# Two state space stages with one scan per unit instead of two and the product a unit ahead, and the preparation around them rearranged

## The chip, the cores and the metric

The kernel runs on one core of a Trainium2 chip. The metric is the device time of one execution in microseconds (us): the median of three runs before is 2466.05 us, from 2464.59 to 2468.78.

The core has five engines with a queue each: TensorE (PE, with its weight loads shown as PEld), VectorE (DVE), ScalarE (ACT), GpSimd (POOL) and SyncE (SP), which here issues the DMAs. Matmul results land in PSUM, eight banks of 128 partitions by 512 floats; everything else is in SBUF.

## The reference, cut to what matters

A stack of 16 layers works on x, 4 batches by 512 positions by 128 channels in float32; each adds f(layernorm(x)) to x. The order is L0a, L0f, L0b, L0f, L1a, L1f, L1b, L1f, L2a, L2f, L2b, L2f, L3a, L3f, L3b, L3f. Three places matter here.

L2b and L3b are state space layers (256 inner channels, 16 states each):

```python
xi, z = in_proj(x)                       # 256 + 256 channels
u = silu(causal_conv4(xi) + conv_b)
dtr, Bc, Cc = split(u @ x_proj)          # 64, 16, 16
delta = softplus(dtr @ dt_proj + dt_proj_b)
A = -exp(A_log)
def step(h, inp):                        # over the 512 positions
    d_t, b_t, c_t, u_t = inp
    dA = jnp.exp(d_t[:, :, None] * A)
    h = dA * h + (d_t * u_t)[:, :, None] * b_t[:, None, :]
    y = jnp.einsum('bdn,bn->bd', h, c_t)
    return (h, y)
y = (y + u * D) * silu(z)
return y @ out_proj
```

L0b is an attention with 16 heads of 8 that weighs all keys once, takes the mean weight of every key over all queries, keeps the 391 keys of 512 with the largest mean (the last 64 always) and attends again over these alone. L2f is a mixture of experts, and L3f a small gated layer; the two are touched only where they hold the beginning of the state space layer that follows.

## The kernel before

Everything is written out in Python, engine by engine. A matmul with `pin=True` and an instruction in `keep(...)` stay in the order in which they are written on their engine; others can be moved by the scheduler between those. The line numbers are those of the profile.

**The loop of L2b and L3b** (`mamba`, L2143). A unit holds 16 inner channels with their 16 states: 8 channels by 16 states fill the 128 partitions, and the two halves t = 0 and 1 lie side by side, each with 512 positions. A batch has 16 units (the two groups c of 128 channels, 8 units each), and a stage 64, numbered n over the four batches. For each unit:

- `fetch` (L2262): two DMAs on SP's queue copy delta from DRAM into a `da` tile, every row of 512 positions spread to 16 partitions. It runs five units ahead, into one of six tiles.
- `decay` (L2273): two ACT instructions make exp(delta * A) in `da`, three units ahead. For the first three units delta comes from PE (`spread`) through a PSUM bank instead of a DMA.
- `gain` (L2284): four matmul records on PE spread delta * u into two PSUM banks, `ps_du`, one unit ahead; there are two such pairs.
- `scan` (L2291): on DVE the product of `ps_du` with B (L2293, 128 x 1024), and then one scan for each half (L2298, 128 x 512), h = da * h + ps_du, from zero; then on GpSimd the product with C (L2301, 128 x 1024), which for the very last unit is on DVE.
- `read` (L2305): every second round, for two units, eight matmul records gather the states into `ps_y`, four units behind.
- `gated` (L2325) on DVE multiplies a group's `ps_y` with silu(z); `output` (L2328) projects a batch back, and `add_to_x` (L440) adds it and takes the moments of the next layernorm.

PSUM holds two pairs of `ps_du`, two banks of tag y and two of tag mm, the last for all other matmuls.

**The preparation of a batch** (`prepare`, L2166) makes u, silu(z), delta, delta * u, B and C of the next batch while this one runs. It is a generator: the loop takes one piece of it in a round (L2363), from round 1 for batch 1 and from two rounds before the end of a batch's 16 for the others. Four pieces are the convolution; then come u and the first half of the gate, the projection to dtr, and one piece with both softplus halves on ACT and eight products of 128 x 512 on GpSimd (L2242) with the DMAs of delta to DRAM behind each four; then B, C and the second half of the gate.

**The first batch** is prepared in the layer before (`mamba_ahead`, L1973): in L2f by a table of rounds (L1943 to L1967), in L3f by hand at its end (L2764 to L2791). `step`, `log` and `rest` are the softplus of one half c; `self.late` lists what runs inside the loop's first rounds instead. In L2f the spare tiles for it are quarters of `xn`, in L3f the second set of batch tiles. `norm` is `roots` (a Sqrt on ACT and a reciprocal) and `centred` (L393, four instructions of 128 x 128 on DVE per batch). `prime` loads an ACT table by a dummy instruction.

**L0b** (L745). In 68 rounds the first pass runs: `weights(n)`, and behind it `importance(n - 4)`, which sums the weights of the keys. `choose(0)` (L879) picks the keys of the first two batches in 16 steps on DVE (a max of 8 and a replace each, L897 and L899), one in a round by a pattern of the round numbers, and sends a mask into the rows of `k` by DMA. `largest(n, i)` (L912) takes the largest score of the second pass (a matmul and a `tensor_reduce`, L925, with four i to a tile n); `into_q` (L974) puts the maxima of four tiles into `q`. In rounds 64 to 66 the first three tiles run; the rest is the start of `stream`, the list of the second pass, whose `weigh` needs `into_q`.

Of the kernel before, what the change touches and what calls it, by code (L numbers as in the profile page):

```python
# [11 lines left out]
F32 = mybir.dt.float32  # L12
# [6 lines left out]
P = 128  # L19
# [255 lines left out]
class Net:  # L275
# [469 lines left out]
    def L0b(self):  # L745
# [7 lines left out]
        with ExitStack() as es:  # L753
# [178 lines left out]


# [12 lines left out]
            AHEAD = 3  # L946
            for n in range(64 + LATE):
# [7 lines left out]
                if 64 <= n < 64 + AHEAD:  # L955
                    for i in range(4):
                        largest(n - 64, i)
# [7 lines left out]
                if n < 36 or n % 7 < 4:  # L965
                    next(choice, None)
            for _ in choice:
                pass
            choice = choose(1)

            def into_q(n):  # L974

                b, g, _ = split(n)
                nm = nmt[n // 4 % 2]
                pt = bank("ps_t", (P, CB, P))
                for j in range(CB):
                    self.tr(pt[:, j], nm[:, j].rearrange("p i r -> p (i r)"))  # L980
                qb = q[g][:, b * S : b * S + S]
                keep(
                    nc.vector.tensor_tensor(qb, qb, pt.rearrange("p j t -> p (j t)"), ALU.add)  # L983
                )
# [75 lines left out]
            LAG = 5  # L1060
            stream = [(largest, n, i) for n in range(AHEAD, LAG) for i in range(4)]
# [19 lines left out]

            plan.at(4 * (4 - AHEAD) + 4, into_q, 3)
            for m in range(len(stream) + 20):
                plan.run(m)
                if m < len(stream):
                    f, n, i = stream[m]
                    f(n, i)
                    if f is largest and i == 3:
                        next(choice, None)
# [807 lines left out]
    def L2f(self):  # L1897
# [3 lines left out]
        with (  # L1901
# [36 lines left out]
            if f:  # L1938

                def bank(name):  # L1940
# [4 lines left out]
                    for at, n, *a in (  # L1945
# [8 lines left out]
                        (30, "step", 1),  # L1954
                        (30, "log", 0),
                        (30, "log", 1),
                        (31, "rest", 0),
                        (32, "rest", 1),
                        (34, "br"),
                        (35, "cr"),  # L1960
                        (37, "gate", 0),
                        (38, "gate", 1),
# [5 lines left out]
                self.late = ((0, f["norm"], 3, 4), (2, f["turn"], 3))  # L1968
# [4 lines left out]
    def mamba_ahead(self, g, spare):  # L1973
# [21 lines left out]
        if spare:  # L1995

            e0, w0, l0, e1 = (
                self.xn[:, CB * b : CB * b + CB].rearrange("p j d -> p (j d)") for b in range(B)
            )
        else:  # L2000
            m["sets"][1] = self.mamba_set(sp, 1)
            e0, w0, l0, e1 = (m["sets"][1][i][:, c] for i in range(2) for c in range(2))
        e, wl, ln = (e0, e1), (w0, sz[:, 0]), (l0, sz[:, 1])
# [65 lines left out]
        def step(c, bank):  # L2069
# [5 lines left out]
            keep(nc.scalar.activation(e[c], ps, AF.Abs, bias=db))  # L2075
            keep(nc.scalar.activation(e[c], e[c], AF.Exp, scale=-1.0))

        def log(c, bank):


            keep(nc.scalar.activation(ln[c], e[c], AF.Ln, bias=ones[:, 0:1]))
            keep(nc.vector.tensor_scalar(wl[c], e[c], 1.0, None, ALU.add))
            keep(
                nc.vector.scalar_tensor_tensor(
                    wl[c], wl[c], 1.0, e[c], ALU.subtract, ALU.subtract
                )
            )

        def rest(c, bank):
            for o, x, y, op in (  # L2090
                (ln[c], ln[c], wl[c], ALU.subtract),
                (dl[:, c], dl[:, c], ln[c], ALU.add),
# [17 lines left out]
            "log": log,  # L2110
# [32 lines left out]
    def mamba(self, g):  # L2143

        nc, tc = self.nc, self.tc
        LAG, AHEAD, FETCH = 4, 3, 5
        with ExitStack() as es:
# [13 lines left out]
            def bank(name):  # L2163
                return pp.tile([P, S], F32, tag="mm", name=name, bufs=2)

            def prepare(b):  # L2166
# [4 lines left out]
                for c in range(2):  # L2171
# [7 lines left out]
                    yield  # L2179

                def gate():
                    raw = rp.tile([P, 2, S], F32, tag="t", name="raw")
                    for c in range(2):
                        ps = bank("ps_z")
                        self.mm(
                            ps,
                            w["in"][:, 256 + c * P : 256 + c * P + P],
                            xT[:, xb : xb + S],
                            pin=True,
                        )  # L2190
                        nc.scalar.copy(raw[:, c], ps)
                        if c == 0:
                            yield
                    nc.scalar.activation(sz, raw, AF.Silu)
                    yield

                nc.scalar.activation(u, raw, AF.Silu)
                gates = gate()
                next(gates)
# [17 lines left out]
                yield  # L2217

# [15 lines left out]
                nc.scalar.activation(w1, w1, AF.Identity, bias=ones[:, 1:2])  # L2234
                for c in range(2):
                    for o, x, y, op in (
                        (w1, w1, e, ALU.subtract),
                        (ln, ln, w1, ALU.subtract),
                        (dl, dl, ln, ALU.add),
                        (du, dl, u, ALU.mult),  # L2240
                    ):
                        nc.gpsimd.tensor_tensor(o[:, c], x[:, c], y[:, c], op)  # L2242
                    nc.sync.dma_start(dram[b][:, c], dl[:, c])
                yield
                yield
                project(br, 64, P)
# [598 lines left out]
```

## Time and profile before

| what | us |
|---|---|
| median of three runs (2464.59 to 2468.78) | 2466.05 |
| the profiled execution, in all | 2471.9 |
| its span in the trace | 2470.2 |
| PE, DVE, ACT, POOL busy in the span | 2183.7, 1751.5, 1307.5, 608.9 |
| L0b, about 498 to 943 | 445 |
| L2f before L2b, 1435 to 1616 | 181 |
| L2b, 1616 to 1875 | 259 |
| L3f before L3b, 2106 to 2169 | 63 |
| L3b, 2169 to 2431 | 262 |

The chain that ended last gives 61% of the span to PE and 26% to DVE, by lines 9.6% to the scans of L2298 and 4.1% to the product of L2293. In the 40 slices PE is at 7 to 9 tenths nearly everywhere, which tells little, since its ends are modelled; DVE is at 9 only in the two state space stages, and GpSimd too is busiest there.

How to read the lines below: a group's line has busy time, the mean of one in ns, and the idle time of the engine before them with what ended it. A timeline line has the start, the duration, and in brackets the idle time before it. A line of windows has the stretch, its length, and the busy time of PE, PEld, DVE, ACT and POOL, then the granted clock of PE and the share and rate of the DMAs. A wait's line has who waited for whom, the total, the times and the longest.

### The profile page before, as it was taken

How to read it: one execution, taken by the hardware profiler on the slowest of the kernel's cores; microseconds unless marked ns; L12 is line 12 of the kernel's file. 1: busy time of each engine (PE TensorE's matmuls, PEld its weight loads, DVE VectorE, ACT ScalarE, POOL GpSimd, SP SyncE). 2: the span in 40 equal slices, each digit the busy share in tenths (PEclk: the TensorE clock that was granted, in tenths of full speed). 3: DMA queues.
4: the chain of work that ended last, by engine and by line, in shares of the span. 5: the costliest groups of instructions: out<-in, count | busy, mean ns of one | idle time of the engine just before them, and what ended most of it. 6: DMA issues, size and time to landing. Idle time of an engine off the chain costs nothing.

```text
span 2470.2 us, 32491 instructions
## 1 busy us (share of the span) xinstructions
PE 2183.7 (88%) x11647; PEld 1025.6 (42%) x11647; DVE 1751.5 (71%) x3544; ACT 1307.5 (53%) x2561; POOL 608.9 (25%) x431
## 2 busy tenths in 40 slices
PE   7999999999899998899877789888868998888867
PEld 2343334733233443567434345442214566422213
DVE  6666666689887675656464674579997557589995
ACT  4555554279645555342442464667635445478642
POOL 1100010010000001022152410048761015148761
PEclk9999999999799999999867889999979999989888
DMA  3000002300000000510200033235542420045540
GB/s 141 1 1 1 1 1 68 72 1 1 2 1 2 1 1 1 112 27 7 100 1 1 0 67 75 56 111 162 148 125 56 87 48 2 1 119 153 152 131 17
DMA packets 68304, 126.79 MB, mean 51 GB/s; under 512 B 9264, under 2 KB 13360, under 8 KB 67504
## 3 DMA queue, kind: packets, MB, share of 16 engines
q1 hardware_dynamic: 68144, 124.73, 19.4%
q8 instruction: 92, 1.51, 0.2%
q14 instruction: 68, 0.56, 0.1%
HBM read 118.93 MB, written 5.64 MB: 50 GB/s over the span
## 4 chain that ended last, share of the span: by engine, by line
PE 61%; DVE 26%; ACT 5%; DMA 3%; issue 2%; POOL 1%; SPq 0%; DVEq 0%; POOLq 0%; ACTq 0%
PE ps_o L346 13%; PE ps_s L346 11%; DVE hc L2298 10%; PE ps_st L346 5%; PE ps_c L346 4%; PE ps L346 4%; DVE ps_du L2293 4%; PE ps_g L346 4%; PE ps_u L346 2%; PE ps_v L346 2%; PE ps_x L346 2%; PE ps_qk L346 2%; DVE xn L393 2%; DVE e L839 2%; PE ps_q L346 2%
## 5 line engine op out<-in xcount | busy, mean ns | idle before, releaser
L2301 POOL TENSOR_TENSOR hc<-hc,cr 128x1024 f32<-128x1024 f32 x126 | 296.0, 2362 | 202.3 <-DVE hc L2298 134.7
L2298 DVE TENSOR_TENSOR_SCAN hc<-da,ps_du 128x512 f32<-128x512 f32 x256 | 298.2, 1206 | 15.6 <-ACT da L2282 2.6
L346 PE MATMUL ps_s<-k,q 32*128 32x512 f32 (+3 forms) x1088 | 275.8, 611 | 16.5 <-DVE mx L839 8.6
L346 PE MATMUL ps_du<-du,spread 64*128 64x512 f32 x512 | 167.5, 730 | 100.3 <-DVE hc L2298 97.9
L538 ACT ACTIVATE e<-ps_s,mx 128x512 f32<-128x512 f32 x256 | 172.6, 686 | 139.9 <-DVE mx L533 133.3
L2282 ACT ACTIVATE da<-da,am 128x512 f32<-128x512 f32 x244 | 165.3, 716 | 96.6 <-DMA da<-dram 82.5
L925 DVE TENSOR_REDUCE nm<-ps_s 128x1 f32<-128x512 f32 x256 | 160.4, 683 | 69.6 <-PE ps_s L346 67.8
L346 PE MATMUL ps<-xT,w_L2f 128*128 128x512 f32 (+1 forms) x416 | 197.1, 621 | 4.0 <-DVE t L1932 4.0
L1007 ACT ACTIVATE e<-ps_st 128x512 f32<-128x512 f32 x256 | 135.3, 601 | 104.9 <-PE ps_s L346 92.4
L533 DVE TENSOR_REDUCE mx<-ps_s 128x2 f32<-128x1024 f32 x128 | 150.9, 1219 | 43.8 <-PE ps_s L346 43.6
L346 PE MATMUL ps_st<-q,k 32*128 32x512 f32 x512 | 167.3, 632 | 6.5 <-DVE q L983 5.5
L2293 DVE TENSOR_TENSOR ps_du<-ps_du,br 128x1024 f32<-128x1024 f32 x128 | 154.8, 1210 | 12.4 <-PE ps_du L346 12.4
L850 ACT ACTIVATE e<-e,mx 128x512 f32<-128x512 f32 (+3 forms) x256 | 140.2, 549 | 20.6 <-DVE mx L839 20.0
L346 PEld LDWEIGHTS ps_s<-k,q 32*128 32x128 f32 x1088 | 96.5, 198 | 113.1 <-DVE mx L839 52.7
L346 PEld LDWEIGHTS ps_du<-du,spread 64*128 64x128 f32 x512 | 46.0, 209 | 214.2 <-DVE hc L2298 184.5
L346 PE MATMUL ps_s<-q,k 64*128 64x512 f32 x512 | 129.1, 618 | 2.2 <-ACT e L538 1.7
L346 PE MATMUL ps_c<-e,vz 128*64 128x512 f32 x512 | 123.5, 604 | 0.8 <-POOL vz L549 0.8
L1932 DVE SCALAR_TENSOR_TENSOR t<-ps,w_L2f,t 128x512 f32<-128x512 f32 (+1 forms) x104 | 76.8, 746 | 63.5 <-PE ps L346 44.4
L346 PEld LDWEIGHTS ps<-xT,w_L2f 128*128 128x128 f32 (+1 forms) x416 | 76.6, 193 | 101.4 <-issue 75.2
L839 DVE CUSTOM_DVE_ANT_0 e<-ps_s,tri 128x512 f32<-128x512 f32 (+3 forms) x256 | 109.6, 484 | 10.1 <-PE ps_s L346 10.1
L1931 ACT ACTIVATE t<-ps,w_L2f 128x512 f32<-128x512 f32 (+1 forms) x104 | 69.7, 682 | 87.3 <-PE ps L346 84.4
L549 POOL TENSOR_TENSOR vz<-v,z 128x512 f32<-128x512 f32 x32 | 33.4, 1043 | 322.0 <-DVE z L547 293.0
(505 smaller groups left out, 4235.1 us busy)
## 6 DMA issues: line engine op xcount, KB each, us to landing
da<-dram SPq DMA_DIRECT2D x244, 256.0 KB
wt<-dram SPq DMA_DIRECT2D x144, 128.0 KB
wt<-dram SPq DMA_DIRECT2D x32, 256.0 KB
dram<-dl SPq DMA_DIRECT2D x16, 256.0 KB
wt<-dram SPq DMA_DIRECT2D x16, 224.0 KB
wt<-dram SPq DMA_DIRECT2D x16, 192.0 KB
wt<-dram SPq DMA_DIRECT2D x16, 160.0 KB
w_L2f<-w_L2f SPq DMA_DIRECT2D x1, 2433.0 KB
```

Of the source, the lines that this page charges most:

```text
L346: i = self.nc.tensor.matmul(out, lhsT, rhs, start=start, stop=stop)
L533: nc.vector.tensor_reduce(mx, sc, AX.X, ALU.max, negate=True)
L538: nc.scalar.activation(es[n][:, hh], sc[:, hh], AF.Exp, bias=mx[:, hh : hh + 1], accum_out=z[m][:, j, hh : hh + 1],)
L839: red = nc.vector.tensor_tensor_reduce(e[:, i, :w], sc[i][:, :w], tri[:, S - w :], -1.0, BIG, ALU.add, ALU.min, mx[:, i : i + 1],)
L850: nc.scalar.activation(e[:, i, :w], e[:, i, :w], AF.Exp, bias=mx[:, i : i + 1], scale=-1.0, accum_out=z[:, i : i + 1],)
L925: nc.vector.tensor_reduce(nm[:, j, i, 9:10], sc, AX.X, ALU.max, negate=True)
L1007: keep(nc.scalar.activation(es_[n][:, i], sc, AF.Exp))
L1932: nc.vector.scalar_tensor_tensor(t[:n], p3[:n], b3[:n, m : m + 1], t[:n], ALU.add, ALU.mult)
L2282: keep(nc.scalar.activation(da[n][:, t], src, AF.Exp, scale=am[:, at : at + 1]))
L2293: nc.vector.tensor_tensor(dx[n], dx[n], sets[b % 2][4].unsqueeze(1).to_broadcast([P, 2, S]), ALU.mult)
L2298: nc.vector.tensor_tensor_scan(hc[n][:, t], da[n][:, t], dx[n][:, t], 0.0, ALU.mult, ALU.add)
L2301: (nc.vector if n == 16 * B - 1 else nc.gpsimd).tensor_tensor(hc[n], hc[n], sets[b % 2][5].unsqueeze(1).to_broadcast([P, 2, S]), ALU.mult)
```

## The change

In the loop, `product` is taken out of `scan` and issued for unit n + 1 ahead of scan n; `gain` runs two units ahead, and there are three pairs of `ps_du`. The two scans become one over 1024 positions: the six `da` tiles are made once, the first position of their second half is set to zero, and the DMA and the exponential leave it out (511 positions), so that the state begins anew there. mm and y have one PSUM bank each. Two units instead of three are spread by PE. The last `roots` of L2b and all `centred` calls move ahead of the loops.

`prepare` has 16 pieces: B before the softplus, GpSimd's products one to a piece with C, the gate and its silu between them, the DMA of a half behind its third product, and delta * u as the last two. The loop takes two pieces in rounds 0, 2, 4, 6 and 8, none in round 1, and one otherwise; later batches begin four rounds before the end of a batch.

In L2f the softplus of both halves is joined (`exps`, `logs`) and spread over rounds 30 to 41. In L0b `choose(0)` has a faster pattern, the first five tiles of `largest` run in rounds 62 to 66 with `into_q(3)` among them, and `choose(1)` makes its first part before the stream and goes on from stream position 16.

```diff
+                if 62 <= n < 62 + LAG:
+                    largest(n - 62, 0)
+                    if n == 66:
+                        into_q(3)
+                    for i in range(1, 4):
+                        largest(n - 62, i)
...
-                if n < 36 or n % 7 < 4:
+                if n < 36 or n % 3 < 2:
                     next(choice, None)
...
             choice = choose(1)
+            next(choice)
...
-            stream = [(largest, n, i) for n in range(AHEAD, LAG) for i in range(4)]
+            stream = []
...
-                    if f is largest and i == 3:
+                    if f is largest and i == 3 and m >= 16:
                         next(choice, None)
...
-                        (30, "step", 1),
-                        (30, "log", 0),
-                        (30, "log", 1),
-                        (31, "rest", 0),
-                        (32, "rest", 1),
-                        (34, "br"),
-                        (35, "cr"),
-                        (37, "gate", 0),
-                        (38, "gate", 1),
+                        (31, "step", 1),
+                        (32, "br"),
+                        (33, "exps"),
+                        (34, "cr"),
+                        (36, "logs"),
+                        (37, "rest", 0),
+                        (38, "rest", 1),
+                        (40, "gate", 0),
+                        (41, "gate", 1),
...
-                self.late = ((0, f["norm"], 3, 4), (2, f["turn"], 3))
+                self.late = ((2, f["turn"], 3),)
...
+        def exps(bank):
+            keep(nc.scalar.activation(e, e, AF.Exp, scale=-1.0))
+            self.prime(AF.Silu)
+
+        def log(e, wl, ln, by_act=False):
+            if by_act:
+                keep(nc.scalar.activation(wl, e, AF.Identity, bias=ones[:, 0:1]))
+            else:
+                keep(nc.vector.tensor_scalar(wl, e, 1.0, None, ALU.add))
+            keep(nc.scalar.activation(ln, e, AF.Ln, bias=ones[:, 0:1]))
+            keep(nc.vector.scalar_tensor_tensor(wl, wl, 1.0, e, ALU.subtract, ALU.subtract))
+
+        def logs(bank):
+            log(e, wl, ln)
+            self.prime(AF.Silu)
...
-        LAG, AHEAD, FETCH = 4, 3, 5
+        LAG, SPREAD, AHEAD, FETCH = 4, 2, 3, 5
...
-                return pp.tile([P, S], F32, tag="mm", name=name, bufs=2)
+                return pp.tile([P, S], F32, tag="mm", name=name)
...
+                steps = (
+                    (w1, w1, e, ALU.subtract),
+                    (ln, ln, w1, ALU.subtract),
+                    (dl, dl, ln, ALU.add),
+                )
                 for c in range(2):
-                    for o, x, y, op in (
-                        (w1, w1, e, ALU.subtract),
-                        (ln, ln, w1, ALU.subtract),
-                        (dl, dl, ln, ALU.add),
-                        (du, dl, u, ALU.mult),
-                    ):
+                    for k, (o, x, y, op) in enumerate(steps):
                         nc.gpsimd.tensor_tensor(o[:, c], x[:, c], y[:, c], op)
-                    nc.sync.dma_start(dram[b][:, c], dl[:, c])
-                yield
-                yield
-                project(br, 64, P)
-                yield
-                project(cr, 192, P)
-                yield
-                for _ in gates:
+                        if k == 2:
+                            nc.sync.dma_start(dram[b][:, c], dl[:, c])
+                        if (c, k) == (0, 1):
+                            project(cr, 192, P)
+                        if (c, k) == (0, 2):
+                            gate(1)
+                        if (c, k) == (1, 0):
+                            nc.scalar.activation(sz, z, AF.Silu)
+                        yield
+                for c in range(2):
+                    nc.gpsimd.tensor_tensor(du[:, c], dl[:, c], u[:, c], ALU.mult)
                     yield
...
+            ring = [sp.tile([P, 2, S], F32, name=f"da{n}") for n in range(6)]
+            for t in ring:
+                nc.gpsimd.memset(t[:, 1, 0:1], 0.0)
+            da = {n: ring[n % 6] for n in range(16 * B)}
...
-                        da[n][:, t],
-                        dram[b][8 * m : 8 * m + 8, c].unsqueeze(0).to_broadcast([16, 8, S]),
+                        da[n][:, t, t:],
+                        dram[b][8 * m : 8 * m + 8, c, t:].unsqueeze(0).to_broadcast([16, 8, S - t]),
...
-                dx[n] = pp.tile([P, 2, S], F32, tag="du", name="ps_du", bufs=2)
+                dx[n] = pp.tile([P, 2, S], F32, tag="du", name="ps_du", bufs=3)
...
+            def product(n):
+                br = sets[n // 16 % 2][4].unsqueeze(1).to_broadcast([P, 2, S])
+                keep(nc.vector.tensor_tensor(dx[n], dx[n], br, ALU.mult))
+
             def scan(n):
-                b = n // 16
-                nc.vector.tensor_tensor(
-                    dx[n], dx[n], sets[b % 2][4].unsqueeze(1).to_broadcast([P, 2, S]), ALU.mult
-                )
                 hc[n] = rp.tile([P, 2, S], F32, name="hc", bufs=7)
-                for t in range(2):
-                    nc.vector.tensor_tensor_scan(
-                        hc[n][:, t], da[n][:, t], dx[n][:, t], 0.0, ALU.mult, ALU.add
-                    )
+                h, a, x = (t.rearrange("p t s -> p (t s)") for t in (hc[n], da[n], dx[n]))
+                keep(nc.vector.tensor_tensor_scan(h, a, x, 0.0, ALU.mult, ALU.add))
...
+            if g == "L2b":
+                self.roots(B - 1, B, keep)
+            self.prime(AF.Exp)
             gain(0)
-            for n in range(AHEAD):
-                da[n] = rp.tile([P, 2, S], F32, name="da", bufs=6)
-                decay(n)
-            for n in range(AHEAD, FETCH):
+            decay(0)
+            gain(1)
+            product(0)
+            if g == "L2b":
+                self.centred(B - 1, keep)
+            decay(1)
+            for n in range(SPREAD, FETCH):
                 fetch(n)
+            decay(2)
...
+            pace = {0: 2, 1: 0, 2: 2, 4: 2, 6: 2, 8: 2}
             for n in range(16 * B + 10):
                 if n + FETCH < 16 * B:
                     fetch(n + FETCH)
+                if n + 1 < 16 * B:
+                    product(n + 1)
                 if n < 16 * B:
                     scan(n)
-                if n + 1 < 16 * B:
-                    gain(n + 1)
+                if n + 2 < 16 * B:
+                    gain(n + 2)
                 if n + AHEAD < 16 * B:
                     decay(n + AHEAD)
-                b, k = divmod(n + 2, 16)
+                b, k = divmod(n + 4, 16)
                 if k == 0 and 1 < b + 1 < B:
                     ahead = prepare(b + 1)
-                if n >= 1:
+                for _ in range(pace.get(n, 1)):
                     next(ahead, None)
...
-                        plan.at(n if last else n + 2, gated, m // 16, m // 8 % 2)
+                        plan.at(n if last else n + 1, gated, m // 16, m // 8 % 2)
...
                 f["step"](0, bank)
+                self.centred(2, keep)
                 f["log"](0, bank)
...
                 f["cr"](bank)
+                self.centred(3, keep)
                 f["turn"](1, bank)
                 self.late = (
-                    (0, lambda bank: self.centred(2, keep)),
                     (0, f["step"], 1),
-                    (0, f["log"], 1),
-                    (0, f["rest"], 1),
-                    (1, lambda bank: self.centred(3, keep)),
+                    (1, f["log"], 1),
+                    (1, f["rest"], 1),
                     (2, f["turn"], 2),
-                    (3, f["turn"], 3),
-                    (4, f["gate"], 0),
-                    (5, f["gate"], 1),
+                    (4, f["turn"], 3),
+                    (5, f["gate"], 0),
+                    (6, f["gate"], 1),
                 )
```

## The prediction

> **What bounds the kernel now.** I read the 40 slices first (counted from 0, DVE is at 9 tenths in slices 27 to 29 and 36 to 38, the two state space stages), then the costliest groups, then DVE's timeline inside a stage, then the waits.
>
> ```profile
> L2298 DVE TENSOR_TENSOR_SCAN hc<-da,ps_du 128x512 f32<-128x512 f32 x256 | 298.2, 1206 | 15.6 <-ACT da L2282 2.6
> L2293 DVE TENSOR_TENSOR ps_du<-ps_du,br 128x1024 f32<-128x1024 f32 x128 | 154.8, 1210 | 12.4 <-PE ps_du L346 12.4
> ```
>
> The product and the scans have almost no idle time before them: DVE sets the pace of both loops. The timeline (start, duration) gives a unit, first in steady state, then in a place where the order happened to differ:
>
> ```profile
> 1664.68 1.21 DVE L2293 TENSOR_TENSOR ps_du<-ps_du,br 128x1024 f32<-128x1024 f32 x1
> 1666.02 2.33 DVE L2298 TENSOR_TENSOR_SCAN hc<-da,ps_du 128x512 f32<-128x512 f32 x2
> 1668.27 1.21 DVE L2293 TENSOR_TENSOR ps_du<-ps_du,br 128x1024 f32<-128x1024 f32 x1
> ...
> 1839.16 1.23 DVE L2293 TENSOR_TENSOR ps_du<-ps_du,br 128x1024 f32<-128x1024 f32 x1
> 1840.30 4.54 DVE L2298 TENSOR_TENSOR_SCAN hc<-da,ps_du 128x512 f32<-128x512 f32 x4
> 1844.76 1.21 DVE L2293 TENSOR_TENSOR ps_du<-ps_du,br 128x1024 f32<-128x1024 f32 x1
> ```
>
> A unit takes 1668.27 - 1664.68 = 3.59: from product to its own scan 1.34, scans to next product 2.25. At 1839 the scan behind the product belongs to an earlier one, and the step is 1.14; the four scans take 4.46, or 2.23 a pair.
>
> The other engines, by windows (length, then PE, PEld, DVE, ACT, POOL busy, clock), and PE's waits in the first of the loops:
>
> ```profile
> 1684.55:1865.60 181.05, 138.31 (x514) 38.82 (x512) 175.89 (x181) 101.39 (x136) 132.77 (x65) 0.86 0.45 131
> 2198.00:2242.00 44.00, 37.00 (x127) 10.46 (x129) 37.91 (x34) 38.07 (x49) 31.38 (x19) 0.96 0.49 137
> PEld ps_du L346 <- DVE hc L2298: 93.0, 49, 3.6
> ```
>
> From unit 16 on only DVE is full (97%). PE waits for a scan at 49 of 64 units, 1.9 us each: that is its slack. At the start of the second loop ACT (87%) is as full as DVE, and DVE stalls.
>
> **Part 1, the loops from unit 16 to 62.** The product of unit n+1 now stands before scan n, so no scan follows its own product: 1.14 in place of 1.34. One scan of 1024 replaces two of 512; no row shows one. From rows: a 1024 product is 1.210 and a 512 one (gated, L2326) 0.675, so a fixed 0.14 and 0.535 per 512; a 512 scan is 1.206, so 1.066 of streaming; a joint one 2.13 + 0.14 = 2.27, and less the overlap of 0.09 (1.206 against 1.115 from start to start) 2.18 to the next start. Bounds: 2.13 (streaming alone) and 2.25 (nothing gained). I take 2.18. New unit 1.14 + 2.18 = 3.32, or 0.27 less. 94 units in the two loops; in some 12 of them gated or a moments instruction already stands between product and scan, and they gain 0.05: 82 x 0.27 + 12 x 0.05 = **-22.7** (bounds -16 and -27).
>
> [...]
>
> **Part 2, what that cover hides no longer.** PE: mm and y banks fall from two to one each, since three products need six. A matmul into mm now waits until ACT has emptied it (0.6 to 0.7 by L2176, L2191, L2214; 1.3 more if a pair of decays stands before it on ACT). Behind that matmul, in PE's order, stand read and the next gain, and DVE's next product waits for gain. Cover: 1.9 per unit. In a batch's eight busy units (1739.8 to 1768.4 of PE's timeline) gain takes 1.06, each projection or convolution piece 1.9 to 1.98, read 1.06 in every second unit: some 28.5 us, against 8 x 3.59 = 28.7 now and 8 x 3.32 = 26.6 then. It is 1.9 short, about one unit's slack; at the reduced clock seen at 1785 (gain 2.08, not 1.13) more. Four such batches: **+4** (0 to +14).
>
> ACT needs 42.6 per 60.3 in a whole batch, 80% of the new 53. GpSimd needs 16 x 2.36 + 8 x 1.28 = 48.0 of 53.1; spreading its 8 preparation products one to a unit keeps hc's backlog near 8 x 0.32 = 2.6, where they ran 10 us in one piece. A piece that waits for ACT's softplus chain holds hc products behind it, and read on PE, four units late by design (13 us), waits for those. On SP the writes of dl stand among the fetches and wait for GpSimd; a fetch issued at 1728.67 landed at 1732.25 for a scan at 1748.19, 14 us of cover. The rows of 511 elements, four bytes off, have no row: even twice the 3.6 us stays under it. All three at 0.
>
> **Part 3, start of the first loop.** Scan 0 starts at 1620.93 and scan 16 at 1684.55, 63.6 for 16 x 3.59 + 0.6 = 58.0. Gain(1) stood on PE behind six spreading matmuls and their evictions (product 1 waited 4.8); now it follows gain(0), and two units are spread, not three. Roots moves ahead of the loop: moments end at 1617.99, then a Sqrt load 1.28, 0.30, an Exp load 1.28, prime 0.20, both decays 1.3: scan 0 at 1622.5. Scan 16 at 1622.5 + 53.1 + 0.6 = 1676.2, a gain of 8.3. The preparation runs two pieces in units 0, 2, 4, 6 and 8, so some stall comes back: **-6** (0 to -8).
>
> **Part 4, start of the second loop.** Scan 0 at 2170.93, scan 16 at 2243.41: 72.5, 14.5 over 58.0. Where it goes:
>
> ```profile
> 2173.18 3.19 DVE L393 TENSOR_SCALAR xn<-x,ln_mv,ln_rs 128x128 f32<-128x128 f32 x4
> 2180.89 2.37 DVE L393 TENSOR_SCALAR xn<-x,ln_mv,ln_rs 128x128 f32<-128x128 f32 x1
> 2216.33 1.23 DVE L2293 TENSOR_TENSOR ps_du<-ps_du,br 128x1024 f32<-128x1024 f32 x1 [3.18 <-PE ps_du L346]
> ```
>
> Eight centred instructions take 7.1 there beside GpSimd (four take 1.09 where GpSimd is idle, 2159.64). They move before the loop, 1.1 into a wait of 1.42 for ACT and 1.1 into one of 1.37 for PE: nothing, or +2.2 without that cover. The waits for PE (1.32, 0.15, 1.36, 3.18) come from ACT, where convolution, softplus and the late gates change tables at 1.28 a load; the same work now falls into fewer units. I leave 8 of stall: 53.7 + 8 = 62, **-10** (-4 to -16).
>
> **Part 5, the selection in L0b.** Sixteen max and replace steps end at round 58, not 63, so the mask's DMA lands before the maxima that need it; maxima start two rounds sooner, and into_q comes before the last three.
>
> ```profile
> PE ps_s L346 <- DMA k<-mask: 4.9, 1, 4.9
> PE ps_st L346 <- DVE q L983: 4.5, 1, 4.5
> ```
>
> DVE is busy 17.6 of the 22.2 us from 664.00 to 686.19, and its work stays: at most 4.6 there and 2.2 at 688.34 can go. **-5** (0 to -7).
>
> **Part 6, the preparation in L2f.** PE waited 0.64 + 0.56 + 3.96 + 0.52 between 1543 and 1561, then ran 8 matmuls in 5.44, where 3.43 is usual:
>
> ```profile
> 1559.43 1.16 PE L346 MATMUL ps<-xT,w_L2f 128*48 128x512 f32 x2 [3.96 <-DVE t L1932]
> ```
>
> ACT was busy 17.2 of 20. Five table loads become four, pairs of 512 become one of 1024, over ten rounds instead of five. 5.7 + 2.0 is there to be had: **-4** (0 to -7).
>
> [...]
>
> The tail of both loops keeps its order: 0 (-3 to +3, as centred of the next stage may fall beside GpSimd).
>
> **Sum.** -22.7 + 4 - 6 - 10 - 5 - 4 = -43.7. The profiled execution spans 2470.2, of 2471.9 in all, and lies 5.85 over the median; the changed span would be 2426.5, and the median 2466.05 - 44 = **2422**.
>
> **The rivals.** *Only the joint scan pays* (the gap behind the product stays as it is in another order). For it: 1.34 may include work that the product needs anyway. Against: 1.14 at 1839.16, and scan to product 1.12. Parts 3 and 4 lose 16 x 0.2 each: -43.7 + 18.0 + 6.4 = -19, 2447. *The starts give nothing*, as ACT, already 87% full, gets the same work in fewer units: -43.7 + 16 = -28, 2438. For it, ACT's window; against, the 7.1 of centred that leaves DVE. *PE serialised behind the single bank*, the slower side: in six batches eight uses of mm each wait for a pair of decays and an eviction, 1.33 + 0.69 = 2.0, with PE full and no slack: 48 x 2.0 = 96, so up to 2518. It decides from 22 such waits on (44/2.0); with 30 the time is 2482. For it: the missing 1.9 per batch. Against: ACT is idle 80 of 181 us, and ran four units ahead at 1728 to 1736. *The change doesn't do what it says* (the joint scan carries state over): excluded, the first factor of its second half is a constant zero.
>
> **How the numbers follow.** Forecast 0.55; only the joint scan 0.15; the starts 0.17; PE 0.13. Less than 0.2% (4.9 us, about what a measurement of this kernel can tell from no change) is left within the edges of PE's case and the first rival: same 0.03. Faster 0.86, slower 0.11. The forecast's own ends (-68 with every part at its best, -4 at its worst) seldom meet; I take 2400 to 2450, which takes in the faster rivals and leaves out most of PE's.
>
> **What would show it.** Steady units 3.32 apart, product to next scan 1.14; a 1024 scan near 2.27; scan 0 to 16 near 54 and 62; no wait for the mask; DVE's idle before the product by PE under 12 us in each loop. Units of 3.5 mean the first rival; waits of PE for ACT in tens of us mean the last.

## The result, and the profile after

No difference: 2470.97 us median of 12 runs (2465.55 to 2474.92) against 2468.69 of 12 runs of the kernel before beside them, ratio 1.0006, 95% interval 0.9994 to 1.0017. The forecast was 2422. The profiled execution takes 2474.54, its span 2472.6.

The costliest groups of the page for the two instructions of the loop:

```profile
L2323 DVE TENSOR_TENSOR_SCAN hc<-da,ps_du 128x1024 f32<-128x1024 f32 x128 | 291.1, 2276 | 0.0
L2318 DVE TENSOR_TENSOR ps_du<-ps_du,br 128x1024 f32<-128x1024 f32 x128 | 155.3, 1213 | 40.6 <-PE ps_du L346 39.2
```

The joint scan takes 2.276, and nothing waits before it. The wait is before the product, and it has gone from 12.4 to 39.2 us. In steady state the timeline shows the unit that was forecast, 1837.33 - 1834.02 = 3.31:

```profile
1834.02 2.27 DVE L2323 TENSOR_TENSOR_SCAN hc<-da,ps_du 128x1024 f32<-128x1024 f32 x1
1836.21 1.21 DVE L2318 TENSOR_TENSOR ps_du<-ps_du,br 128x1024 f32<-128x1024 f32 x1
1837.33 2.27 DVE L2323 TENSOR_TENSOR_SCAN hc<-da,ps_du 128x1024 f32<-128x1024 f32 x1
```

Where the rest went, by the starts of scans and of the last addition to x of each stage (L443), in us:

| | before | after |
|---|---|---|
| end of L2f, ahead of the first loop | 1616.05 | 1604.60 |
| first loop, end to end | 256.2 | 260.4 |
| of it scan 0 to 16 | 63.6 | 66.6 |
| of it scan 16 to 62 | 173.9 | 177.6 |
| second loop, end to end | 281.7 | 291.0 |
| of it scan 0 to 16 | 72.5 | 79.9 |
| of it scan 16 to 62 | 173.9 | 177.6 |

The stages ahead of the first loop gave 11.4 in this pair of profiles. The loops became 13.5 longer, although two units in three (43 of 63 steps from scan to scan in each loop) take under 3.4 us. Between scan 0 and scan 62 of both loops DVE's time splits into its waits (the brackets of its timeline) and the rest, its own work:

| us, both loops | before | after |
|---|---|---|
| scan 0 to scan 62 | 484.0 | 501.7 |
| of it waits | 11.5 | 64.3 |
| of it the rest | 472.4 | 437.4 |

So DVE's own work became 35 shorter and its waits 53 longer. All of the changed kernel's waits are for PE; the largest groups, first loop and second loop:

```profile
DVE ps_du L2318 <- PE ps_du L346: 14.8, 9, 5.3
DVE x L443 <- PE ps_o L346: 9.5, 3, 4.9
...
DVE ps_du L2318 <- PE ps_du L346: 22.3, 9, 7.7
DVE x L443 <- PE ps_o L346: 9.4, 3, 5.1
```

The timeline of the first loop, units 8 and 9, has one of the places that pay (a bracket holds the idle time before, and what ended it):

```profile
1639.50 1.98 PE L346 MATMUL ps_d<-u,w_L2b 128*128 128x512 f32 x4
...
1643.66 1.28 ACT L2304 ACT_TABLE_LOAD   x1
...
1644.95 1.33 ACT L2304 ACTIVATE da<-da,am 128x512 f32<-128x512 f32 x2
1646.19 0.56 ACT L2226 COPY cr<-ps_d 128x512 f32<-128x512 f32 x1
...
1646.81 1.24 PE L346 MATMUL ps_z<-xT,w_L2b 128*128 128x512 f32 x2 [4.27 <-ACT cr L2226]
1647.97 1.93 PE L346 MATMUL ps_y<-hc,gather 128*32 128x512 f32 x8
...
1649.84 2.60 PE L346 MATMUL ps_du<-du,spread 64*128 64x512 f32 x8
...
1651.62 1.23 DVE L2318 TENSOR_TENSOR ps_du<-ps_du,br 128x1024 f32<-128x1024 f32 x1 [5.28 <-PE ps_du L346]
```

The projection for C ends near 1641.5. Its copy out of the one mm bank stands on ACT behind the end of the softplus chain, a table load and a pair of decays, and is done at 1646.75. PE waits 4.27 with ps_z, which needs that bank; ps_y and the next ps_du stand behind ps_z in PE's order, and DVE waits 5.28 for ps_du. The longest of PE's waits for ACT's evictions in this loop:

```profile
PE ps_z L346 <- ACT cr L2226: 9.0, 3, 4.3
PE ps_dt L346 <- ACT e L2244: 4.1, 3, 1.4
PE ps_d L346 <- ACT z L2208: 2.3, 3, 0.9
```

In the kernel before the same view has only one wait for an eviction, 2.2 us behind the first decays. Over both loops PE's waits for ACT add up to some 41 us, and to 6 in the kernel before.

### The profile page after: what moved, and what is told of

Read it like the earlier page. It is cut to its first block, busy times and chain, and to the rows that moved or that the text cites. A ratio compares the mean times of both kernels' runs of the same rounds, so it can differ in the third digit from the quotient of the medians.

```text
span 2472.6 us, 32674 instructions
## 1 busy us (share of the span) xinstructions
PE 2188.7 (89%) x11639; PEld 1031.9 (42%) x11639; DVE 1731.2 (70%) x3413; ACT 1307.3 (53%) x2563; POOL 611.3 (25%) x443
## 4 chain that ended last, share of the span: by engine, by line
PE 65%; DVE 16%; ACT 8%; issue 7%; DMA 2%; POOL 1%; SPq 1%; POOLq 0%; DVEq 0%; ACTq 0%
PE ps_o L346 13%; PE ps_s L346 10%; PE ps_st L346 5%; PE ps_c L346 4%; PE ps L346 4%; PE ps_g L346 4%; PE ps_x L346 3%; DVE hc L2323 2%; PE ps_du L346 2%; PE ps_u L346 2%; PE ps_v L346 2%; DVE e L839 2%; PE ps_qk L346 2%; PE ps_q L346 1%; PE ps_tr L351 1%
## 5 line engine op out<-in xcount | busy, mean ns | idle before, releaser
L2323 DVE TENSOR_TENSOR_SCAN hc<-da,ps_du 128x1024 f32<-128x1024 f32 x128 | 291.1, 2276 | 0.0
L346 PE MATMUL ps_s<-k,q 32*128 32x512 f32 (+3 forms) x1088 | 278.2, 595 | 11.4 <-DVE mx L839 8.6
L346 PE MATMUL ps_du<-du,spread 64*128 64x512 f32 x512 | 175.8, 766 | 81.0 <-DVE hc L2323 77.7
L2318 DVE TENSOR_TENSOR ps_du<-ps_du,br 128x1024 f32<-128x1024 f32 x128 | 155.3, 1213 | 40.6 <-PE ps_du L346 39.2
L659 DVE TENSOR_TENSOR hc<-hc,wt 128x1024 f32<-128x1024 f32 x80 | 94.7, 1188 | 24.0 <-ACT hc L1936 12.2
```

Of the source, the lines that this page charges most:

```text
L346: i = self.nc.tensor.matmul(out, lhsT, rhs, start=start, stop=stop)
L659: nc.vector.tensor_tensor(h, h, wt[b, k][:, r:e], ALU.mult)
L2318: keep(nc.vector.tensor_tensor(dx[n], dx[n], br, ALU.mult))
L2323: keep(nc.vector.tensor_tensor_scan(h, a, x, 0.0, ALU.mult, ALU.add))
```

## The experiments

Three theories. **T1**: the addition to x stands too early in DVE's order and waits for output matmuls of its own unit (4.92 at scan 24). The change puts the addition, its moments and the gating product in `keep(...)`, where the scheduler could move them before. **T2**: the one mm bank makes PE wait for ACT, and DVE for PE, wherever the work stands. **T3**: two preparation pieces in a unit overload PE and ACT at the loops' starts. All ratios below are to the kernel before.

**The addition two units later.**

```diff
-    plan.at(n + 4, output, m // 16)
+    plan.at(n + 4, output matmuls, m // 16)
+    plan.at(n + 6, add_to_x, m // 16)
```

> The changed kernel with one edit: the addition to x (and the moments behind it) is issued two units after the output matmuls that feed it, no longer in their unit (batches 0 to 2 of both loops); the matmuls stay where they are. Theory T1 (the addition stands too early in VectorE's order and waits for output matmuls of its own unit; profile of after: 4.92 + 3.68 + 0.86 us in the first loop, 5.09 + 3.38 + about 0.9 in the second, some 19 in all) expects these waits gone and nothing in their place: 2452 to 2458 us, ratio 0.992 to 0.995. Theory T2 (TensorE itself is late behind ScalarE's evictions of its one bank, wherever the addition stands) expects the wait to move to the next product: ratio 0.997 to 1.000.

2462.17 us, 0.9972 (0.9956 to 0.9987): 8 us less than the changed kernel, about half of what T1 expected. In the second loop the steps to scans 24, 25 and 26 are now 3.33, 4.04 and 5.61 (the last with 2.3 of the addition's own time), 13.0 for 17.4; in the first loop to scans 40 to 42 they are 16.3 for 16.0: there the wait went to the next products. Both theories hold in part. Whether the addition without `keep` would have done the same wasn't run.

**The pieces moved.**

```diff
-    pace = {0: 2, 1: 0, 2: 2, 4: 2, 6: 2, 8: 2}
+    pace = {0: 2, 1: 0, 2: 2, 9: 2, 10: 2, 11: 2}
```

> The changed kernel with the units in which the first batch of each loop is prepared by two pieces moved: from units 0, 2, 4, 6 and 8 to 0, 2, 9, 10 and 11, so that units 3 to 8 issue one piece each (all 16 must be issued by unit 11). Theory T3 (two pieces in a unit overload ScalarE and TensorE in units 4 to 9) expects the waits of units 6, 7 and 9 in the first loop (3.10 + 3.02 + 1.97 over the step) and 4, 6, 7, 8 in the second (3.0 + 4.6 + 4.2 + 7.8) to fall by half: 10 to 14 us, ratio 0.994 to 0.996. T2 expects the waits to be moved to later units with the pieces: ratio 0.998 to 1.001. Loss is possible if the delta rows of batch 1 then land too late for unit 16.

2465.07 us, 0.9971 (0.9953 to 0.9989). The page's wait of the product for ps_du falls from 39.2 to 29.8. 9 us less than the changed kernel by the ratios, short of T3's 10 to 14, and part of the waits did move with the pieces: the step to scan 11 of the first loop is 8.01 where it was 3.30.

**One bank each in the kernel before.**

```diff
-    return pp.tile([P, S], F32, tag="mm", name=name, bufs=2)
+    return pp.tile([P, S], F32, tag="mm", name=name)
-    yp[c] = pp.tile([P, S], F32, tag="y", name="ps_y", bufs=2)
+    yp[c] = pp.tile([P, S], F32, tag="y", name="ps_y")
```

> The kernel before with one work bank and one y bank in place of two each, the gating product one unit earlier and three late pieces of the second loop moved by one or two units as in the changed kernel; two scans, product and scan in one unit, old pace. T2 expects the loops of before to lose what the banks cost: VectorE's waits for ps_du from 12 us to 25 to 40, ratio 1.005 to 1.012. T1 and T3 expect 0.999 to 1.002. This kernel has more slack in a unit (3.59 us against 3.31), so a smaller loss than in the changed kernel is possible under T2 too.

2521.73 us, 1.0203 (1.0184 to 1.0223): 50 us, far over T2's own 12 to 30. (In the second loop three late pieces also stand a unit later, as in the changed kernel; the first loop has only the banks and the gating product, and loses 23 of the 50.) By the additions to x the first loop takes 279.1 (256.2 before) and the second 308.8 (281.7). The timeline ahead of scan 25 of the first loop:

```profile
1725.38 1.33 ACT L2282 ACTIVATE da<-da,am 128x512 f32<-128x512 f32 x2
...
1725.53 3.78 PE L346 MATMUL ps_d<-u,w_L2b 128*128 128x512 f32 x4 [3.94 <-ACT br L2214]
1729.24 1.43 PE L346 MATMUL ps_y<-hc,gather 128*32 128x512 f32 x8
...
1730.60 2.05 PE L346 MATMUL ps_o<-w_L2b,y 128*128 128x128 f32 x16
...
1732.69 0.69 DVE L443 TENSOR_TENSOR x<-x,ps_o 128x512 f32<-128x512 f32 x1 [5.10 <-PE ps_o L346]
```

It is the same chain as in the changed kernel: PE waits 3.94 for the bank, everything behind it is late, and DVE stands 5.10 before the addition.

Not all of the 50 carries over. The step from scan 0 to scan 1 takes 15.82 and 15.13 where it took 8.47 and 7.15: here three units are spread by PE, one half after another, through the one bank, while the changed kernel spreads two, half of them through the y bank, and has steps of 3.31 and 8.28. Without these 15 the bank costs 35.

**One y bank alone.** The second line of that diff without the first (with the gating product one unit earlier, as there).

> The kernel before with one y bank in place of two, and the gating product one unit earlier, as in the changed kernel; two work banks stay. T2 in the form that the work bank is what costs expects 1.000 to 1.005, so that nearly all of the 2.0% of one bank each is the work bank; if the y bank and the early gating are as much to blame: 1.008 to 1.012.

2471.03 us, 0.9998 (0.9986 to 1.0009). The y bank and the early gating cost nothing; the 50 us are the mm bank's, but for what the three late pieces cost.

**The stages ahead alone.** The changed kernel with `mamba` and the late lists of before.

> The changed kernel with the loop function of before (two scans, product and scan together, 2 ps_du pairs, 2 work banks, 2 y banks, old pace and old late lists), so that of the change only the parts ahead of the two loops are left: selection in L0b, preparation in L2f and L3f. All theories expect the parts ahead of the first loop to keep their 11.5 us (1616.05 to 1604.60 in the profiles). The additive account (one banks cost 50 in the loops, shorter units give 36 back, the stages ahead 11) expects 2455 to 2460 us, 0.9945 to 0.9965 of before; a theory in which the loop's loss comes from the new stages ahead (L2f and L3f leave work to the loop's start) expects 1.000.

2456.57 us, 0.9947 (0.9930 to 0.9965): 13 us, between 9 and 17. The changed kernel's loops thus give back what its new stages ahead bring.

**The same loop with banks to spare.** Three kernels leave out the summing of y over the states:

```diff
-    read(m)
-    y = yp[c] * sz
+    y = u * sz
```

The first is the changed kernel otherwise; the second gives the bank that this frees to mm (bufs=2); the third has the new stages ahead and the loops of before, with two mm banks.

> The changed kernel with the summing of y over the states left out (the skip and gather matmuls into ps_y; the gate multiplies u in its place), so that TensorE has some 20 us less to do in each loop and the y bank is not needed; one work bank as in the changed kernel. It is the reference for the next two. T2 expects it slower than the two bank kernel beside it by 25 to 50 us; if the bank matters only through the y matmuls that queue behind it, under 10.

> The same with y summing left out, and the bank that this frees given to the work tiles: two work banks, three ps_du pairs, product a unit ahead, joint scans, all in PSUM as in the changed kernel. T2 expects 25 to 50 us under noread_one_bank. Against noread_before_loops it shows what shorter units are worth where banks are not short: the prediction's sum of loop terms (22.7 + 6 + 10) says 35 to 39 us; if the shorter unit were no gain, 0.

> The new stages ahead with the loops of before (two scans, product in its unit, two work banks), y summing left out in the same way. With T2 and the prediction's unit price, 30 to 39 us above noread_two_banks and near noread_one_bank (within 15 us either way); with a theory in which the joint scan and the product ahead bring nothing in the loop, equal to noread_two_banks.

2466.32 us (0.9987, 0.9970 to 1.0004), 2437.41 (0.9870, 0.9855 to 0.9885) and 2470.48 (0.9996, 0.9977 to 1.0015). In the changed loop the second bank is worth 29 us; with two banks the changed loop is 33 us faster than the old one. Both lie where T2 put them, but the 33 is not the price of the loop. The gating product now reads u and silu(z), both in SBUF, where it read PSUM. Its rows with the stages ahead alone, in the third kernel and in the second:

```profile
L2342 DVE TENSOR_TENSOR y<-ps_y,sz 128x512 f32<-128x512 f32 x16 | 10.8, 675 | 3.5 <-PE ps_y L346 3.5
L2342 DVE TENSOR_TENSOR y<-u,sz 128x512 f32<-128x512 f32 x16 | 32.9, 2058 | 0.4 <-ACT sz L2056 0.4
L2351 DVE TENSOR_TENSOR y<-u,sz 128x512 f32<-128x512 f32 x16 | 20.1, 1254 | 0.0
```

Of the 33, 13 are this product's (32.9 - 20.1). Against the old loops with y in place (2456.57) the second kernel is 19 faster. For the first kernel no trace comparable with these shows this product, so the 29 may hold some of it too.

**Banks to spare without leaving out work.** The product goes to SBUF, so that two ps_du pairs do, and mm and y have two banks again:

```diff
-    keep(nc.vector.tensor_tensor(dx[n], dx[n], br, ALU.mult))
+    keep(nc.vector.tensor_tensor(hc[n], dx[n], br, ALU.mult))
-    keep(nc.vector.tensor_tensor_scan(h, a, x, 0.0, ALU.mult, ALU.add))
+    keep(nc.vector.tensor_tensor_scan(h, a, h, 0.0, ALU.mult, ALU.add))
```

> The changed kernel with the product written into SBUF (the tile of hc, 8 of them, over which the joint scan then runs in place), so that ps_du needs 2 pairs of PSUM banks and the work bank and the y bank are 2 each again, as before; y is one tile in SBUF. Orders of all engines as in the changed kernel. Theory T2 (the single work bank makes TensorE wait for ScalarE's evictions, and VectorE for TensorE) expects VectorE's waits for ps_du to fall from 39 us to about 12 and the waits of the additions by half, together 25 to 40 us: ratio 0.984 to 0.990, if product and scan cost the same (1.21 and 2.28 us) from SBUF. Theory T1 (place of the addition) and T3 (pace of the pieces) expect at most 5 us: ratio 0.998 to 1.000. A scan that is slower in place would show in its row, not in the waits.

2574.69 us, 1.0416 (1.0399 to 1.0433). The product's wait fell to 20.6, but the scan rose from 2276 ns to 3118, 128 x (3118 - 2276) = 108 us in all:

```profile
L2323 DVE TENSOR_TENSOR_SCAN hc<-da,hc 128x1024 f32<-128x1024 f32 x128 | 398.9, 3118 | 1.2 <-ACT da L2304 1.2
```

As a test of T2 it says nothing; what it shows is told at the end.

**The dt piece split.** One dt projection in a unit, where the second had to wait for two reads (relu, abs) of the first one's bank (the two products delta * u become one piece in turn):

```diff
     nc.scalar.activation(e[:, c], ps, AF.Abs, bias=db)
+    if c == 0:
+        yield
```

> The changed kernel with one edit: the piece that issues both dt projections is split, one projection in a unit (to keep 16 pieces, the two du products are one piece). T2 in its narrower form: the place where the one bank costs most is that piece, in which the second dt matmul waits until ScalarE has read the first dt bank twice (relu and abs), and the next matmuls for ps_du and ps_y stand behind it. It expects the waits before the gating product and the next product in units 21 and 37 (in all some 2 us each, 4 places) and part of units 6 to 9 of both loops gone: 10 to 20 us, 0.992 to 0.996 of the changed kernel, so 0.993 to 0.997 of before. If the wait merely moves to the next piece: 0.999 to 1.002 of before.

2459.93 us, 0.9957 (0.9942 to 0.9973). The steps to scans 21 and 37 fall from 6.64 and 5.57 to 3.90, which is the gating product's own share. But the pieces behind are a unit later, so that the second half of the gate meets the output matmuls in one unit, and the step to scan 24 grows from 10.64 to 12.06:

```profile
1690.82 2.07 PE L346 MATMUL ps_z<-xT,w_L2b 128*128 128x512 f32 x2 [2.62 <-ACT cr L2226]
1692.83 1.74 PE L346 MATMUL ps_y<-hc,gather 128*32 128x512 f32 x8
...
1694.50 2.05 PE L346 MATMUL ps_o<-w_L2b,y 128*128 128x128 f32 x16
...
1696.59 0.69 DVE L443 TENSOR_TENSOR x<-x,ps_o 128x512 f32<-128x512 f32 x1 [6.35 <-PE ps_o L346]
```

**The takers of the bank spread out.** One bank and three pairs as in the changed kernel, with all of these edits: the split, output a unit later and the addition two units behind it, other units for the pieces and for the second loop's late gates:

```diff
-    pace = {0: 2, 1: 0, 2: 2, 4: 2, 6: 2, 8: 2}
+    pace = {0: 0, 1: 2, 2: 2, 8: 2, 10: 2, 11: 2}
-    (5, f["gate"], 0),
-    (6, f["gate"], 1),
+    (10, f["gate"], 0),
+    (11, f["gate"], 1),
-    plan.at(n + 4, output, m // 16)
+    plan.at(n + 5, output matmuls, m // 16)
+    plan.at(n + 7, add_to_x, m // 16)
```

> The changed kernel with its three du pairs and one work bank, and the takers of that bank spread out: dt in two pieces, pieces doubled in units 1, 2, 8, 10 and 11 (none in unit 0, so that the late step of the second loop's set 0 comes ahead of the convolution), the late gates of the second loop in units 10 and 11 (before 5 and 6), the output matmuls one unit later and the addition to x two units behind them. If T1, T2 and T3 each hold and their waits are separate, the sum of the single edits (late addition 8, pace 7, split 10 to 20, first unit and gates 5 to 10) gives 2430 to 2445 us, 0.983 to 0.990 of before; if all of them treat the same wait, 2455 to 2462, 0.995.

2435.21 us, 0.9858 (0.9836 to 0.9879): 35 us faster than the kernel before, and the best kernel of these. The loops take 246.3 and 269.6, 22.0 less than before in all. The product's row on the page:

```profile
L2320 DVE TENSOR_TENSOR ps_du<-ps_du,br 128x1024 f32<-128x1024 f32 x128 | 155.4, 1214 | 26.1 <-PE ps_du L346 25.4
```

And DVE's waits for ps_du in the first loop (total, times, longest):

```profile
DVE ps_du L2320 <- PE ps_du L346: 11.7, 10, 3.8
```

Ten waits in 64 units are left in that loop, none over 3.8, and by the starts of scans the units 16 to 62 of the first loop take 171.5 (1663.49 to 1834.94) for 177.6. Between scan 0 and scan 62 of both loops DVE's own work is as short as in the changed kernel (436.9), and its waits fall from 64.3 to 31.3. PE still waits some 34 us for ACT there, for 41 in the changed kernel: most of its stalls remain, and fewer of them reach DVE.

**Evictions ahead of the decays.** As the last, with a unit's piece issued before its decays.

> spread_out with one more edit: within a unit the preparation's piece is issued ahead of the decays, so that ScalarE reads the work bank before it takes up decays that may wait for their delta rows (ScalarE stood 65.6 us before decays for the transfer in spread_out, and an eviction behind them keeps the bank). T2 expects the product's waits for ps_du to fall from 25 us to 10 to 18 and 2422 to 2432 us, 0.980 to 0.984 of before; if decays then come late for their scans instead, 2435 to 2450.

2438.47 us, 0.9880 (0.9863 to 0.9896): no gain over spreading. The product's wait falls to 16.1 as expected, but the scan, which waited for nothing, now waits 9.5 for GpSimd to give tiles of hc free.

## Why the prediction was wrong

**Part 1 was right, in DVE's own work.** A unit of 3.31 (3.32 forecast), product to scan 1.12 (1.14), scan to product 2.19 (2.18), a joint scan of 2.276 (2.27). From scan 16 to scan 62 the two loops without DVE's waits take 327.7 where they took 347.2: 19.5 for a forecast of 22.7. The rows that the forecast went by hold: a scan behind a product that it doesn't depend on starts 0.2 sooner (1.12 for 1.34).

**Part 2 failed, and with it the sum.** It took +4, at most +14, for the single banks. The runs put the mm bank at 35 us in the loops of before (50 with the first steps) and at about 29 in the changed loop, and the changed loops' waits are 53 longer. The step that went wrong is the one that compared PE's work with the shorter units (28.5 us against 26.6) and charged the 1.9 that is missing. That is a count of throughput; the loss is latency. PE takes its matmuls here in the written order, and each of its stalls at the bank is as long as ACT's queue ahead of the eviction: up to 4.3 us in the first loop behind a softplus chain with its table loads, and 4.9 in the second, where the text priced 2.0, a pair of decays and an eviction.

The cover of 1.9 a unit was read too large as well. The line behind it (93.0, 49) is PEld's, the weight loads, which overlap the matmuls (in the kernel before one of 0.19 at 1767.12 lies inside the ps_d that takes 1.98 from 1766.59 on). PE's own line for the same wait in the first loop of the kernel before is

```profile
PE ps_du L346 <- DVE hc L2298: 46.5, 36, 2.8
```

which is 0.7 a unit over 64 units. Every one of the longer stalls takes more than that.

**Parts 3 and 4** (-6 and -10) rest on the same cover and came out with the other sign: scan 0 to 16 is 66.6 and 79.9, where 53.7 and 62 were forecast. In the first units two pieces of preparation and the late pieces use the bank within one unit, and the softplus chain falls among them. Spread out these units take 57.9 and 69.8, and with two banks and y left out 57.8 and 71.1. So of the first loop's 13 most is the bank's, and the second loop's forecast of 62 fails even without it: 12.6 us of waits for ps_du remain there with two banks. That ACT at 87% would give the starts nothing was a rival, and it was too mild.

**Parts 5 and 6** (-9 together) came out in their sum, 11.4 by the profiles and 13 by the kernel with these parts alone, and hardly one by one. Measured from the last addition to x of the stage ahead to its own last, L0b takes 459.6 to 461.4 in the three traces with the old stages and 449.1 to 453.8 in the ten with the new ones, about twice the 5 of part 5; the waits for the mask and for `into_q` are gone. L2f takes 185.2 to 191.0 and 187.3 to 187.8: the wait of 3.96 went, one of 4.0 for ACT stands before the output matmuls instead, and a gain of 4 isn't shown. That the sum fits is luck. (DVE is at 9 tenths in slice 9 too, in L0b; the text ahead names the two state space stages alone.)

**The sum in the trace's terms.** From scan 0 to scan 62 of the loops DVE's own work -35 and its waits +53, the loops' ends -4, the stages ahead of the first loop -11: some +2 in all, as the spans have it (2470.2 and 2472.6).

**The rivals.** *Only the joint scan pays* took off part 1 what the product ahead is worth there, 82 x (0.27 - 0.05) = 18.0; with product to scan at 1.12 it is excluded. *PE serialised behind the single bank* named the mechanism; its sign came (DVE's waits for ps_du were to stay under 12 us in each loop, and are 14.8 and 24.4), and the point from which it decides, 44 us of waits, lies between what the bank costs and the 53 us by which the waits grew; it was given 0.13 on the ground that ACT is idle 80 of 181 us and ran four units ahead. ACT's mean load says nothing of the moment at which an eviction stands behind a chain. What was not thought of is the place of the addition to x (8 us by the first experiment): by the profile of before it ran a unit later and without a wait, though written in the same place, since there the scheduler could move it.

That the single bank is what mostly costs is shown by taking the second away (before), by giving it back (with y left out) and by spreading its users, which gains 36 with one bank. What each single stall of the changed kernel is worth is not: against the changed kernel the three single edits gain 8, 9 and 12 us by their ratios, all of them move part of the wait, and together with the late gates and the first unit they gain the 36.

## What to carry to other kernels

Price a buffer that goes from two to one by latency, not by load: for each use, what stands on the evicting engine's queue ahead of the eviction, and what stands on the producer's queue behind the one that waits. If buffers are needed elsewhere, spread the users of the single one, one to a unit and none beside a long chain, and issue consumers a unit or two after their producer. A shorter unit also uses up the slack that hid such stalls (PE's waits for scans in the first loop fell from 46.5 us to 36.9 here), so the two are to be weighed together.

## What the runs showed of the hardware

**With both inputs in SBUF the scan took longer beside GpSimd, and GpSimd's products took longer too.** In the kernel with the product in SBUF the first scan, with GpSimd idle, takes 2.28; the next ones take 3.54 to 3.56 (timeline, DVE and GpSimd):

```profile
1607.91 2.28 DVE L2323 TENSOR_TENSOR_SCAN hc<-da,hc 128x1024 f32<-128x1024 f32 x1
...
1610.27 2.36 POOL L2328 TENSOR_TENSOR hc<-hc,cr 128x1024 f32<-128x1024 f32 x1 [7.71 <-DVE hc L2323]
1611.22 3.56 DVE L2323 TENSOR_TENSOR_SCAN hc<-da,hc 128x1024 f32<-128x1024 f32 x1
```

GpSimd ends at 1612.63, the scan at 1614.78, 2.15 later: as if the scan had stood still until GpSimd was done. Over both loops the scans take 3118 ns on average, and GpSimd's products in the first loop 3714 where the changed kernel's take 2361. The changed kernel's scan has one input in PSUM, and there neither is seen: at 1840.64 it takes 2.28 beside a product of 2.36 on GpSimd from 1839.75 on, and over both loops 2276 ns on average. The rows put the price at 108 us here. The gating product of the kernels without y, with both inputs in SBUF too, takes 0.66 us at its shortest and 6.30 at its longest; that GpSimd makes the difference there is not shown.

**Behind a stall PE's granted clock was halved.** In the kernel before with one bank, ps_d takes 3.78 after its wait of 3.94, and 3.78 after one of 4.29 at 1674.45, where it takes 1.98 without a wait at 1666.12. Windows of PE (stretch, length, busy time and records, granted clock, DMA share and rate), shortly ahead of the stall and right after it:

```profile
1715.00:1720.00 5.00, 4.85 (x18) 1.00 0.33 105
1725.50:1729.30 3.80, 3.77 (x8) 0.50 0.00 0
```

In the changed kernel the windows 1646.80 to 1650.00, right behind its wait of 4.27, show a clock of 0.64, and 1652.40 to 1655.00 one of 1.00. Later it is halved in a stretch ahead of which PE's waits were only 1.76 and 2.18, so here no wait as long as 3.94 stood right ahead of it:

```profile
1658.00:1664.00 6.00, 5.50 (x16) 0.50 0.52 149
```

No run here separates the price of the clock from that of the waits.

**With less work on PE its granted clock was lower.** With the y matmuls left out and the old loops, the first loop's windows give (stretch, length, then PE, PEld, DVE, ACT and POOL busy, clock):

```profile
1599.00:1854.00 255.00, 173.41 (x444) 59.01 (x444) 242.59 (x244) 152.71 (x204) 180.59 (x88) 0.74 0.45 132
```

With the y matmuls (the kernel with the stages ahead alone) 721 records take 199.63 in a like stretch, 257.00 from 1600 on, at a clock of 0.89: with 277 records fewer PE was busy only 26 us less. That this kernel isn't faster than the one that does the work (2470.48 against 2456.57) is not the clock's doing, though: DVE waits in these loops no more than there (9.2 us and 11.8 from scan 0 to scan 62), and its gating product takes 22 us more.
